# A four-layer network on one core: one-pass normalizations, biases and expert sums added by GpSimd, and a product of two weight matrices

## The chip, the cores and the metric

One core of one Trainium2 chip runs the whole network as one program. The metric is the device time in microseconds. The engines are named as the profile names them: PE (matrix products; PEld loads their weights), DVE (VectorE), ACT (ScalarE), POOL (GpSimd) and SP (which issues the transfers). PE writes its results to PSUM, in eight banks of 512 columns of float32; POOL works on SBUF only.

## What is computed

x has 4 sequences of 1024 tokens with 128 channels, in float32. Eight blocks follow one another, and each adds to x what it makes of the normalized x:

```
def _layernorm(x, axis=-1, eps=1e-05):
    m = jnp.mean(x, axis=axis, keepdims=True)
    v = jnp.var(x, axis=axis, keepdims=True)
    return (x - m) / jnp.sqrt(v + eps)
...
    x = x + _L0_attn_ref(_layernorm(x, axis=-1), ...)   # delta rule, 8 heads
    x = x + _L0_ffn_ref(_layernorm(x, axis=-1), ...)    # 128 -> 512, sines, relu, 512 -> 128, + b2
    x = x + _L1_attn_ref(_layernorm(x, axis=-1), ...)   # a small MLP trained on k, v; then applied to q
    x = x + _L1_ffn_ref(_layernorm(x, axis=-1), ...)    # 8 experts, all computed, gated
    x = x + _L2_attn_ref(_layernorm(x, axis=-1), ...)   # normalizes once more, then 8 heads
    x = x + _L2_ffn_ref(_layernorm(x, axis=-1), ...)
    x = x + _L3_attn_ref(_layernorm(x, axis=-1), ...)   # 16 heads
    x = x + _L3_ffn_ref(_layernorm(x, axis=-1), ...)    # 8 experts, the best 2
    return x
```

The parts that the change touches, besides the normalizations:

```
_L0_ffn_ref:  return jnp.einsum('bsf,fd->bsd', act, W2) + b2
_L1_attn_ref: q = x @ W_Q
              return silu(q @ W1 + b1) @ W2 + b2        # W1, b1, W2, b2 as trained
_L1_ffn_ref:  for e in range(E):
                  out = out + weights[:, e:e + 1] * (x @ expert_w[e] + expert_b[e])
_L2_attn_ref: xn = (x - mu) * jax.lax.rsqrt(var + LN_EPS) * gamma + beta
```

## The kernel before

x stays in SBUF for the whole program as `self.x`, 128 tokens on the partitions, 32 such tiles of 128 channels. `self.xnT` holds the normalized x with the channels on the partitions; `tok(t, n)` names n of its columns from tile t on.

A normalization runs over 4 batches of 8 tiles (`ln_batch`). For each tile DVE takes the statistics (`bn_stats` and `bn_aggr`, L82 and L83); ACT takes the square root for the 8 tiles (L85), DVE the reciprocal (L86) and the offset (`nm`, L106); then ACT scales the 8 tiles one by one (L109), PE transposes them four to a PSUM bank (L120), and ACT copies each bank to `xnT` (L126). In l2_attn, whose block normalizes a second time, `twice` is set: the scaled tiles go through statistics and scaling again (`xm`), and DVE writes `xnT` with the block's scale and bias (L124). `layernorm` runs the 4 batches with pools of two buffers and four PSUM banks; the two attentions, l0_ffn, l1_attn, l2_ffn and l3_ffn call it. l1_ffn calls `ln_batch` itself, one batch ahead of its tiles.

The first attention, the rounds of l1_attn and the two attentions of layers 2 and 3 have an order written out by hand; all else is put in order by a scheduler, within what the pools' buffers allow. Every engine takes its instructions in that order.

*l0_ffn* goes through 8 groups of 512 tokens. For each of 4 chunks of 128 hidden channels PE makes `hp` (L532), ACT scales it (L536), DVE takes whole turns off (L503, L504), ACT takes the sine (L539), DVE combines (L540), ACT applies relu (L541). Then for each of the 4 tiles PE sums 4 products (L545) and a product of a row of ones with the bias `b2` (L548), and DVE adds the result to x (`add_x`, L129).

*The output of l1_attn* (L601 to L618) begins when the rounds have trained W1, b1, W2 and b2. For each of 8 groups PE makes `qp` (L607), ACT copies it (L609), PE makes `hp` (L611), ACT applies silu (L613), and for each tile PE makes a product and a bias product of one row (L616, L617), and DVE adds to x.

*l1_ffn* makes the gates of 8 tiles at a time (L923 and `weights`), then goes tile by tile (`tile_of`): PE transposes the gates (L969), ACT copies them (L971), PE makes the 8 experts' outputs in two banks (L975, three `ep` banks). DVE adds the first five, each times its gate, onto x one after the other (L984); ACT scales the other three into `sc` (L982), and PE sums them together with the gated biases in `bp`, by a product with the biases (L986) and three with the identity (L988); DVE adds `bp` to x.

Elsewhere POOL adds results to x in l2_attn (L1326), l2_ffn (L1364, L1380) and l3_attn (the output bias, L1411), and clears buffers of the attentions. In the rounds of l1_attn it makes differences (L661), in the first attention products and a bias (L283, L284, L382).

Of the kernel before, what the change touches and what calls it, by code (L numbers as in the profile page):

```python
# [9 lines left out]
F32 = mybir.dt.float32  # L10
AF = mybir.ActivationFunctionType
ALU = mybir.AluOpType
# [3 lines left out]
P = 128  # L16
# [11 lines left out]
class Net:  # L28
# [71 lines left out]
    def ln_batch(self, pool, ps, b, twice=None):  # L100
        nc = self.nc

        def scaled(src, tag):
            mv, rs = self.stats(pool, src, TPB)
            nm = pool.tile([P, TPB], F32, tag="nm", name="nm")
            nc.vector.scalar_tensor_tensor(nm, mv[:, :, 0], -1.0, rs, ALU.mult, ALU.mult)  # L106
            dst = pool.tile([P, TPB, D], F32, tag=tag, name=tag)
            for i in range(TPB):
                nc.scalar.activation(  # L109
                    dst[:, i, :], src[:, i, :], AF.Identity, bias=nm[:, i : i + 1], scale=rs[:, i : i + 1]  # L110
                )
            return dst

        xn = scaled(self.x[:, b * TPB : (b + 1) * TPB, :], "xn")
        if twice is not None:
            xn = scaled(xn, "xm")
        for q in range(TPB // 4):
            tp = ps.tile([P, 4, P], F32, tag="tp", name="tp")
            for i in range(4):
                nc.tensor.transpose(tp[:, i, :], xn[:, 4 * q + i, :], self.ident)  # L120
            dst = self.tok(b * TPB + 4 * q, 512)
            src = tp.rearrange("p a b -> p (a b)")
            if twice is not None:
                nc.vector.tensor_scalar(dst, src, twice[0], twice[1], ALU.mult, ALU.add)  # L124
            else:
                nc.scalar.copy(dst, src)  # L126
# [362 lines left out]
    def l0_ffn_load(self):  # L489
# [6 lines left out]
            b2=self.row("L0_ffn_b2"),  # L496
# [9 lines left out]
    def l0_ffn(self):  # L506
# [5 lines left out]
        with tc.tile_pool(name="f0", bufs=3) as two, tc.tile_pool(name="f0c", bufs=1) as one, tc.tile_pool(  # L512
# [15 lines left out]
            for n in range(NB * SEQ // 512):  # L528
                act = two.tile([P, NF, 512], F32, tag="act", name="act")
                for c in range(NF):  # L530
# [10 lines left out]
                    nc.scalar.activation(act[:, c, :], s, AF.Relu, bias=f["b1"][:, c : c + 1])  # L541
                for i in range(4):
                    op = po.tile([P, D], F32, tag="op", name="op")
                    for c in range(NF):
                        nc.tensor.matmul(  # L545
                            op, lhsT=act[:, c, i * P : (i + 1) * P], rhs=f["W2"][:, c, :], start=c == 0, stop=False
                        )
                    nc.tensor.matmul(op, lhsT=self.ones[0:1, :], rhs=f["b2"], start=False, stop=True)  # L548
                    self.add_x(4 * n + i, op)
# [17 lines left out]
    def l1_attn(self):  # L567
# [32 lines left out]
        with tc.tile_pool(name="l1o", bufs=2) as two, tc.tile_pool(name="l1q", bufs=2, space=PSUM) as ps:  # L600
            b2p = ps.tile([1, D], F32, tag="b2p", name="b2p", bufs=1)  # L601
            nc.tensor.transpose(b2p, B2, self.ident)
            b2r = two.tile([1, D], F32, tag="b2r", name="b2r", bufs=1)
            nc.scalar.copy(b2r, b2p)
            for n in range(NB * SEQ // 512):
                qp = ps.tile([P, 512], F32, tag="qp", name="qp")
                nc.tensor.matmul(qp, lhsT=wq, rhs=self.tok(4 * n, 512), start=True, stop=True)  # L607
                q = two.tile([P, 512], F32, tag="q", name="q")
                nc.scalar.copy(q, qp)  # L609
                hp = ps.tile([P, 512], F32, tag="hp", name="hp")  # L610
                nc.tensor.matmul(hp, lhsT=W1, rhs=q, start=True, stop=True)  # L611
                a = two.tile([P, 512], F32, tag="a", name="a")
                nc.scalar.activation(a, hp, AF.Silu, bias=B1)  # L613
                for i in range(4):
                    op = ps.tile([P, D], F32, tag="op", name="op")
                    nc.tensor.matmul(op, lhsT=a[:, i * P : (i + 1) * P], rhs=W2, start=True, stop=False)  # L616
                    nc.tensor.matmul(op, lhsT=self.ones[0:1, :], rhs=b2r, start=False, stop=True)  # L617
                    self.add_x(4 * n + i, op)  # L618
# [291 lines left out]
    def l1_ffn_load(self):  # L910
# [4 lines left out]
            self.mat("L1_ffn_expert_b"),  # L915
# [23 lines left out]
    def l1_ffn(self):  # L939
# [3 lines left out]
        gw, gb, ew, eb = self.f1  # L943
# [714 lines left out]
```

## Time and profile before

| | us |
|---|---|
| three runs: median (lowest, highest) | 2828.85 (2817.63, 2829.1) |
| the profiled execution | 2815.77 |
| its span | 2814.1 |

| engine | busy us | share of the span |
|---|---|---|
| PE | 2547.2 | 91% |
| DVE | 1829.7 | 65% |
| ACT | 1538.4 | 55% |
| POOL | 179.1 | 6% |

The span holds the eight blocks one after another; stretches of it are named by their start and end in us. A row of a table of stretches gives, for each engine, its busy time and instructions, then the clock granted to PE (1.00 is full) and the transfers. A row of the groups gives the line, the engine, the operation, output and inputs, shapes and count; then busy us and mean ns of one; then the idle time before them and what ended it. A row of the timeline gives start and duration in us first. A busy engine is one with instructions under way: it may be slow at them.

### The profile page before, as it was taken

To read this page: it belongs to the slowest core of one execution; us is meant where nothing else is said; L and a number is where in the kernel's file an instruction comes from. 1 tells how busy PE (TensorE), PEld (TensorE's weight loads), DVE (VectorE), ACT (ScalarE), POOL (GpSimd) and SP (SyncE) were. 2 spreads that over 40 slices of the span, in tenths; PEclk is the share of its full clock that TensorE was granted. 3 is DMA by queue.
4 is the path that set the end of the run, shared out by engine and by line. 5 is a ranking of instruction groups with operands and counts; after the bars stand their busy time and mean duration, and the time that the engine had idled before them with its cause. 6 is when DMAs were issued, how large, how long until landed. Compare 5 with 4: busy or idle time off the path is not lost.

```text
span 2814.1 us, 51848 instructions
## 1 busy us (share of the span) xinstructions
PE 2547.2 (91%) x20320; PEld 1278.6 (45%) x20320; DVE 1829.7 (65%) x3857; ACT 1538.4 (55%) x3486; POOL 179.1 (6%) x301
## 2 busy tenths in 40 slices
PE   5687868999989959999999769999999999999967
PEld 4455536699985523333333343333333333333356
DVE  5999657567663666667676146777776776777134
ACT  4465466655554450656566650666666666666642
POOL 6111000000000000000000050000000000000001
PEclk8698878899998965999999865999999999999968
DMA  2233220000000000000100000000000000000000
GB/s 52 63 87 76 56 59 1 1 1 2 1 2 1 1 1 15 14 13 14 21 13 10 5 0 8 8 8 11 9 9 9 8 12 8 10 8 8 4 9 24
DMA packets 116468, 46.62 MB, mean 17 GB/s; under 512 B 88402, under 2 KB 110843, under 8 KB 116220
## 3 DMA queue, kind: packets, MB, share of 16 engines
q1 hardware_dynamic: 116220, 43.25, 7.8%
q8 instruction: 163, 2.67, 0.4%
q14 instruction: 85, 0.70, 0.1%
HBM read 16.95 MB, written 12.98 MB: 11 GB/s over the span
## 4 chain that ended last, share of the span: by engine, by line
PE 63%; DVE 3%; ACT 2%; POOL 1%; issue 1%; DMA 0%; SPq 0%; POOLq 0%; DVEq 0%; ACTq 0%
PE pb L1183 30%; PE po L1205 15%; PE pa L1158 6%; PE ep L975 2%; PE tp L120 2%; PE pp L1098 1%; PE gp L923 1%; PE bp L988 1%; DVE st L82 1%; ACT xn L109 1%; PE pv L1079 1%; PE op L617 1%; PE rp L1576 0%; PE bp L986 0%; PE op L616 0%
## 5 line engine op out<-in xcount | busy, mean ns | idle before, releaser
L1187 ACT ACTIVATE es<-pb 128x512 f32<-128x512 f32 x1536 | 836.2, 594 | 558.8 <-PE pb L1183 404.2
L1183 PE MATMUL pb<-q,k 32*128 32x512 f32 x3072 | 957.6, 642 | 0.7 <-ACT es L1187 0.7
L1158 PE MATMUL pa<-k,q 32*128 32x512 f32 x3072 | 909.8, 677 | 17.5 <-DMA q<-q 15.7
L1170 DVE TENSOR_REDUCE bm<-pa 128x2 f32<-128x1024 f32 x512 | 625.6, 1225 | 274.3 <-PE pb L1183 169.5
L1205 PE MATMUL po<-es,v 128*32 128x256 f32 (+1 forms) x5760 | 480.0, 405 | 0.0
L1183 PEld LDWEIGHTS pb<-q,k 32*128 32x128 f32 x3072 | 314.7, 184 | 348.2 <-ACT es L1187 190.0
L1166 DVE TENSOR_REDUCE bm<-pa 128x16 f32<-128x1024 f32 x256 | 312.5, 1221 | 107.4 <-PE pb L1183 60.7
L1205 PEld LDWEIGHTS po<-es,v 128*32 128x32 f32 x5760 | 114.2, 108 | 543.1 <-issue 510.5
L1158 PEld LDWEIGHTS pa<-k,q 32*128 32x128 f32 x3072 | 252.3, 193 | 92.8 <-DVE bm L1170 49.5
L120 PE MATMUL tp<-ident,xn 128*128 128x128 f32 x192 | 65.8, 442 | 56.0 <-ACT xn L109 50.1
L319 DVE TENSOR_TENSOR pr<-T,L 128x31 f32<-128x31 f32 (+15 forms) x248 | 90.0, 363 | 27.5 <-DMA L<-ld 20.5
L1212 DVE COPY oT<-po 128x512 f32<-128x512 f32 x48 | 32.7, 682 | 109.1 <-PE po L1205 109.1
L322 DVE TENSOR_TENSOR T<-T,pr 128x31 f32<-128x31 f32 (+15 forms) x248 | 92.3, 372 | 8.5
L109 ACT ACTIVATE xn<-x,nm,rs 128x128 f32<-128x128 f32 x224 | 89.2, 481 | 7.6 <-DVE nm L106 7.6
L984 DVE SCALAR_TENSOR_TENSOR x<-ep,g,x 128x128 f32<-128x128 f32 x160 | 55.1, 348 | 31.3 <-ACT sc L982 21.3
L277 PE MATMUL wide<-bt,kt 32*128 32x128 f32 x512 | 31.4, 375 | 48.0 <-DVE mt L366 34.3
L120 PEld LDWEIGHTS tp<-ident,xn 128*128 128x128 f32 x192 | 34.7, 187 | 88.1 <-ACT xn L109 60.1
L729 ACT ACTIVATE w<-tr,half 128x128 f32<-128x128 f32 x128 | 47.1, 368 | 47.7 <-PE tr L727 44.9
L82 DVE BATCH_NORM_STATS2 st<-x 128x6 f32<-128x128 f32 x256 | 65.2, 265 | 11.5 <-DMA x<-in_L_attn_x_dram 4.0
L704 ACT ACTIVATE a<-hp,wb 128x128 f32<-128x128 f32 x128 | 47.1, 368 | 40.7 <-PE hp L700 39.7
L975 PE MATMUL ep<-L_ffn_expert_w,xnT 128*128 128x512 f32 x128 | 69.1, 629 | 0.0
L1457 POOL MEMSET c<- 128x512 f32 (+1 forms) x2 | 2.3, 1172 | 1021.8 <-PE tp L120 1021.8
(442 smaller groups left out, 3566.5 us busy)
## 6 DMA issues: line engine op xcount, KB each, us to landing
ld<-kk SPq DMA_DIRECT2D x128, 32.0 KB
L<-ld SPq DMA_DIRECT2D x8, 512.0 KB
td<-T SPq DMA_DIRECT2D x8, 512.0 KB
tb<-td SPq DMA_DIRECT2D x128, 32.0 KB
md<-nt SPq DMA_DIRECT2D x192, 2.0 KB
q<-md SPq DMA_DIRECT2D x192, 2.0 KB
x<-in_L_attn_x_dram SPq DMA_DIRECT2D x4, 512.0 KB
od<-o SPq DMA_DIRECT2D x32, 64.0 KB
```

Of the source, the lines that this page charges most:

```text
L82: nc.vector.bn_stats(st, src[:, i, :])
L109: nc.scalar.activation(dst[:, i, :], src[:, i, :], AF.Identity, bias=nm[:, i : i + 1], scale=rs[:, i : i + 1])
L120: nc.tensor.transpose(tp[:, i, :], xn[:, 4 * q + i, :], self.ident)
L319: nc.vector.tensor_mul(pv, T[:, 0 : j + 1, j : j + 1].to_broadcast(sh), L[:, j : j + 1, j + 1 :].to_broadcast(sh))
L322: nc.vector.tensor_sub(T[:, 0 : j + 1, j + 1 :], T[:, 0 : j + 1, j + 1 :], pv)
L975: nc.tensor.matmul(ep.rearrange("p a b -> p (a b)"), lhsT=self.tok(t), rhs=ew[:, 4 * h : 4 * h + 4, :].rearrange("p a b -> p (a b)"), star ...
L1158: nc.tensor.matmul(pa[:, j % 2, :], lhsT=st["q"][r, i * P : (i + 1) * P], rhs=st["k"][r, n * 512 : (n + 1) * 512], start=True, stop=True,)
L1166: nc.vector.tensor_reduce(out[:, :, 1:9], pa.rearrange("p j (c s) -> p j c s", c=8), axis=AX.X, op=ALU.max)
L1170: nc.vector.tensor_reduce(out[:, :, n : n + 1], pa, axis=AX.X, op=ALU.max)
L1183: nc.tensor.matmul(pb, lhsT=st["k"][r, kc * P : (kc + 1) * P], rhs=st["q"][r, n * 512 : (n + 1) * 512], start=True, stop=True,)
L1187: nc.scalar.activation(es[turn][:, j, :], pb, AF.Exp, scale=scale)
L1205: nc.tensor.matmul(po[r, cols], lhsT=vring[b % 2][:, kc, 4 * g + j, :], rhs=es[:, j, cols], start=kc == 0, stop=True, skip_group_check=True,)
```

## The change

`ln_batch` takes the statistics of a tile without `bn_aggr`; the sums and squares of 8 tiles are combined in five operations of 8 columns. Four of the 8 tiles are scaled by POOL and four by ACT. With `twice` there is one pass: the second normalization's factor is worked out from the first one's variance (six more operations of 8 columns), and ACT in place of DVE writes `xnT`.

In l0_ffn and in l1's output POOL adds the bias to four tiles of x at a time (`add_bias`), PE has no bias product, and DVE adds four tiles at once from one PSUM bank (`add_four`). In l1's output W_Q and the trained W1 are multiplied once, and a group has one product where it had two. In l1_ffn the gates of 8 tiles are transposed at once and multiplied with a block-diagonal tile of the expert biases (`biases`, two products and two `add_four` a batch), and POOL adds the three experts that ACT scaled.

```diff
@@ -98,32 +98,59 @@
                 self.ln_batch(pool, ps, b, twice)
 
     def ln_batch(self, pool, ps, b, twice=None):
+
+
         nc = self.nc
-
-        def scaled(src, tag):
-            mv, rs = self.stats(pool, src, TPB)
-            nm = pool.tile([P, TPB], F32, tag="nm", name="nm")
-            nc.vector.scalar_tensor_tensor(nm, mv[:, :, 0], -1.0, rs, ALU.mult, ALU.mult)
-            dst = pool.tile([P, TPB, D], F32, tag=tag, name=tag)
-            for i in range(TPB):
-                nc.scalar.activation(
-                    dst[:, i, :], src[:, i, :], AF.Identity, bias=nm[:, i : i + 1], scale=rs[:, i : i + 1]
-                )
-            return dst
-
-        xn = scaled(self.x[:, b * TPB : (b + 1) * TPB, :], "xn")
-        if twice is not None:
-            xn = scaled(xn, "xm")
-        for q in range(TPB // 4):
+        src = self.x[:, b * TPB : (b + 1) * TPB, :]
+
+        st = pool.tile([P, TPB, 6], F32, tag="st", name="st")
+        for i in range(TPB):
+            nc.vector.bn_stats(st[:, i, :], src[:, i, :])
+        s, d, q, rs = (pool.tile([P, TPB], F32, tag=t, name=t) for t in ("s", "d", "q", "rs"))
+        nc.vector.tensor_sub(d, st[:, :, 1], st[:, :, 4])
+        nc.vector.tensor_add(q, st[:, :, 2], st[:, :, 5])
+        nc.vector.scalar_tensor_tensor(d, d, D / 4.0, d, ALU.mult, ALU.mult)
+        nc.vector.tensor_add(q, q, d)
+        nc.vector.tensor_add(s, st[:, :, 1], st[:, :, 4])
+        if twice is None:
+            nc.scalar.activation(rs, q, AF.Sqrt, bias=self.eps, scale=1.0 / D)
+            nc.vector.reciprocal(rs, rs)
+        else:
+            nc.vector.tensor_scalar(rs, q, 1.0 / D, EPS, ALU.mult, ALU.add)
+            nc.vector.reciprocal(rs, rs)
+            nc.vector.tensor_mul(q, q, rs)
+            nc.vector.tensor_scalar(q, q, 1.0 / D, EPS, ALU.mult, ALU.add)
+            nc.vector.reciprocal(q, q)
+            nc.vector.tensor_mul(rs, rs, q)
+            nc.scalar.activation(rs, rs, AF.Sqrt)
+        nm = pool.tile([P, TPB], F32, tag="nm", name="nm")
+        nc.vector.scalar_tensor_tensor(nm, s, -0.5, rs, ALU.mult, ALU.mult)
+        xn = pool.tile([P, TPB, D], F32, tag="xn", name="xn")
+        for i in range(TPB):
+            sl, bl = rs[:, i : i + 1], nm[:, i : i + 1]
+            if i % 2:
+                nc.gpsimd.tensor_scalar(xn[:, i, :], src[:, i, :], sl, bl, ALU.mult, ALU.add)
+            else:
+                nc.scalar.activation(xn[:, i, :], src[:, i, :], AF.Identity, bias=bl, scale=sl)
+        for n in range(TPB // 4):
             tp = ps.tile([P, 4, P], F32, tag="tp", name="tp")
             for i in range(4):
-                nc.tensor.transpose(tp[:, i, :], xn[:, 4 * q + i, :], self.ident)
-            dst = self.tok(b * TPB + 4 * q, 512)
-            src = tp.rearrange("p a b -> p (a b)")
+                nc.tensor.transpose(tp[:, i, :], xn[:, 4 * n + i, :], self.ident)
+            dst = self.tok(b * TPB + 4 * n, 512)
+            src_ = tp.rearrange("p a b -> p (a b)")
             if twice is not None:
-                nc.vector.tensor_scalar(dst, src, twice[0], twice[1], ALU.mult, ALU.add)
+                nc.scalar.activation(dst, src_, AF.Identity, bias=twice[1], scale=twice[0])
             else:
-                nc.scalar.copy(dst, src)
+                nc.scalar.copy(dst, src_)
+
+    def add_bias(self, t, bias):
+
+        xs = self.x[:, t : t + 4, :]
+        self.nc.gpsimd.tensor_add(xs, xs, bias.unsqueeze(1).to_broadcast([P, 4, D]))
+
+    def add_four(self, t, ps):
+        xs = self.x[:, t : t + 4, :]
+        self.nc.vector.tensor_add(xs, ps, xs)
 
     def add_x(self, t, ps):
         self.nc.vector.tensor_add(self.x[:, t, :], ps, self.x[:, t, :])
@@ -493,7 +520,7 @@
             W2=self.load("L0_ffn_W2", W2.rearrange("(c p) d -> p c d", p=P), [P, 4, D]),
             b1=self.mat("L0_ffn_b1"), th=self.mat("L0_ffn_quantum_phases"),
             wr=self.mat("L0_ffn_quantum_weights_real"), wi=self.mat("L0_ffn_quantum_weights_imag"),
-            b2=self.row("L0_ffn_b2"),
+            b2=self.spread("L0_ffn_b2"),
         )
 
     def turns(self, pool, r, shape):
@@ -539,14 +566,15 @@
                     nc.scalar.activation(s, r, AF.Sin, scale=TWO_PI)
                     nc.vector.scalar_tensor_tensor(s, s, co[:, c : c + 1], hp, ALU.mult, ALU.add)
                     nc.scalar.activation(act[:, c, :], s, AF.Relu, bias=f["b1"][:, c : c + 1])
+                self.add_bias(4 * n, f["b2"])
+                op = po.tile([P, 4, D], F32, tag="op", name="op")
                 for i in range(4):
-                    op = po.tile([P, D], F32, tag="op", name="op")
                     for c in range(NF):
                         nc.tensor.matmul(
-                            op, lhsT=act[:, c, i * P : (i + 1) * P], rhs=f["W2"][:, c, :], start=c == 0, stop=False
+                            op[:, i, :], lhsT=act[:, c, i * P : (i + 1) * P], rhs=f["W2"][:, c, :],
+                            start=c == 0, stop=c == NF - 1,
                         )
-                    nc.tensor.matmul(op, lhsT=self.ones[0:1, :], rhs=f["b2"], start=False, stop=True)
-                    self.add_x(4 * n + i, op)
+                self.add_four(4 * n, op)
 
 
 
@@ -598,24 +626,33 @@
             with tc.If(many > 0):
                 self.l1_steps(kT, vT)
         with tc.tile_pool(name="l1o", bufs=2) as two, tc.tile_pool(name="l1q", bufs=2, space=PSUM) as ps:
-            b2p = ps.tile([1, D], F32, tag="b2p", name="b2p", bufs=1)
+
+            tp = ps.tile([P, D], F32, tag="one", name="tp", bufs=1)
+            nc.tensor.transpose(tp, wq, self.ident)
+            wqT = two.tile([P, D], F32, tag="wqT", name="wqT", bufs=1)
+            nc.scalar.copy(wqT, tp)
+            wp = ps.tile([P, D], F32, tag="one", name="wp", bufs=1)
+            nc.tensor.matmul(wp, lhsT=wqT, rhs=W1, start=True, stop=True)
+            qw = two.tile([P, D], F32, tag="qw", name="qw", bufs=1)
+            nc.scalar.copy(qw, wp)
+            b2p = ps.tile([1, D], F32, tag="two", name="b2p", bufs=1)
             nc.tensor.transpose(b2p, B2, self.ident)
             b2r = two.tile([1, D], F32, tag="b2r", name="b2r", bufs=1)
-            nc.scalar.copy(b2r, b2p)
+            nc.vector.tensor_copy(b2r, b2p)
+            bp = ps.tile([P, D], F32, tag="two", name="bp", bufs=1)
+            nc.tensor.matmul(bp, lhsT=self.ones[0:1, :], rhs=b2r, start=True, stop=True)
+            b2 = two.tile([P, D], F32, tag="b2", name="b2", bufs=1)
+            nc.vector.tensor_copy(b2, bp)
             for n in range(NB * SEQ // 512):
-                qp = ps.tile([P, 512], F32, tag="qp", name="qp")
-                nc.tensor.matmul(qp, lhsT=wq, rhs=self.tok(4 * n, 512), start=True, stop=True)
-                q = two.tile([P, 512], F32, tag="q", name="q")
-                nc.scalar.copy(q, qp)
                 hp = ps.tile([P, 512], F32, tag="hp", name="hp")
-                nc.tensor.matmul(hp, lhsT=W1, rhs=q, start=True, stop=True)
+                nc.tensor.matmul(hp, lhsT=qw, rhs=self.tok(4 * n, 512), start=True, stop=True)
                 a = two.tile([P, 512], F32, tag="a", name="a")
                 nc.scalar.activation(a, hp, AF.Silu, bias=B1)
+                self.add_bias(4 * n, b2)
+                op = ps.tile([P, 4, D], F32, tag="op", name="op")
                 for i in range(4):
-                    op = ps.tile([P, D], F32, tag="op", name="op")
-                    nc.tensor.matmul(op, lhsT=a[:, i * P : (i + 1) * P], rhs=W2, start=True, stop=False)
-                    nc.tensor.matmul(op, lhsT=self.ones[0:1, :], rhs=b2r, start=False, stop=True)
-                    self.add_x(4 * n + i, op)
+                    nc.tensor.matmul(op[:, i, :], lhsT=a[:, i * P : (i + 1) * P], rhs=W2, start=True, stop=True)
+                self.add_four(4 * n, op)
 
     def l1_rounds(self, keep, kT, vT):
 
...
@@ -940,13 +976,18 @@
 
 
         nc, tc = self.nc, self.tc
-        gw, gb, ew, eb = self.f1
+        gw, gb, ew = self.f1
         E, OWN = 8, 5
         with ExitStack() as c:
             ln = c.enter_context(tc.tile_pool(name="f1l", bufs=2))
             lps = c.enter_context(tc.tile_pool(name="f1q", bufs=2, space=PSUM))
             one = c.enter_context(tc.tile_pool(name="f1c", bufs=2))
             two = c.enter_context(tc.tile_pool(name="f1", bufs=3))
+
+            eb = one.tile([TPB * E, TPB, D], F32, tag="eb", name="eb", bufs=1)
+            nc.gpsimd.memset(eb, 0.0)
+            for i in range(TPB):
+                nc.sync.dma_start(eb[E * i : E * i + E, i, :], self.w["L1_ffn_expert_b"])
             ps = c.enter_context(tc.tile_pool(name="f1p", bufs=2, space=PSUM))
 
             def weights(b):
@@ -963,12 +1004,22 @@
                 nc.vector.tensor_mul(g, g, sm.unsqueeze(2).to_broadcast([P, TPB, E]))
                 return g
 
+            def biases(b, g):
+
+                ap = ps.tile([TPB * E, P], F32, tag="ap", name="ap", bufs=1)
+                nc.tensor.transpose(ap, g.rearrange("p t e -> p (t e)"), self.ident)
+                gT = one.tile([TPB * E, P], F32, tag="gT", name="gT")
+                nc.scalar.copy(gT, ap)
+                for n in range(TPB // 4):
+                    bp = ps.tile([P, 4, D], F32, tag="bp", name="bp", bufs=1)
+                    nc.tensor.matmul(
+                        bp.rearrange("p a b -> p (a b)"), lhsT=gT,
+                        rhs=eb[:, 4 * n : 4 * n + 4, :].rearrange("p a b -> p (a b)"), start=True, stop=True,
+                    )
+                    self.add_four(b * TPB + 4 * n, bp)
+
             def tile_of(t, g):
                 xs = self.x[:, t, :]
-                ap = ps.tile([P, P], F32, tag="ap", name="ap", bufs=1)
-                nc.tensor.transpose(ap[0:E, :], g, self.ident)
-                gT = two.tile([E, P], F32, tag="gT", name="gT")
-                nc.scalar.copy(gT, ap[0:E, :])
                 eps = []
                 for h in range(2):
                     ep = ps.tile([P, 4, D], F32, tag="ep", name="ep", bufs=3)
@@ -982,17 +1033,15 @@
                     nc.scalar.mul(sc[:, e - OWN, :], eps[e // 4][:, e % 4, :], g[:, e : e + 1])
                 for e in range(OWN):
                     nc.vector.scalar_tensor_tensor(xs, eps[e // 4][:, e % 4, :], g[:, e : e + 1], xs, ALU.mult, ALU.add)
-                bp = ps.tile([P, D], F32, tag="bp", name="bp", bufs=1)
-                nc.tensor.matmul(bp, lhsT=gT, rhs=eb, start=True, stop=False)
                 for e in range(OWN, E):
-                    nc.tensor.matmul(bp, lhsT=self.ident, rhs=sc[:, e - OWN, :], start=False, stop=e == E - 1)
-                self.add_x(t, bp)
+                    nc.gpsimd.tensor_add(xs, xs, sc[:, e - OWN, :])
 
             self.ln_batch(ln, lps, 0)
             g = weights(0)
             for b in range(NB):
                 if b + 1 < NB:
                     self.ln_batch(ln, lps, b + 1)
+                biases(b, g)
                 for i in range(TPB):
                     tile_of(b * TPB + i, g[:, i, :])
                     if i == TPB // 2 and b + 1 < NB:
```

More of the change, by code (lines that the diff above doesn't have):

```diff
@@ L914, in l1_ffn_load @@
             self.load("L1_ffn_expert_w", ew.rearrange("e d f -> d e f"), [D, 8, D]),
-            self.mat("L1_ffn_expert_b"),
         )
```

## The prediction

> **What bounds the kernel now.** I began with the table of stretches, cut at the stages.
>
> ```profile
> core 0: us, PE busy (x) PEld busy (x) DVE busy (x) ACT busy (x) POOL busy (x), PEclk, DMA share, GB/s
> 403.00:465.00 62.00, 60.60 (x302) 40.92 (x303) 51.12 (x104) 48.18 (x80) 0.00 (x0) 1.00 0.00 1
> 837.00:893.00 56.00, 44.23 (x163) 26.67 (x163) 14.91 (x77) 15.14 (x24) 0.00 (x0) 0.85 0.00 1
> 893.00:1005.00 112.00, 111.87 (x491) 65.47 (x491) 69.50 (x268) 52.37 (x170) 0.00 (x0) 0.92 0.00 1
> 1005.00:1052.00 47.00, 17.36 (x54) 8.56 (x53) 31.86 (x162) 30.73 (x80) 0.69 (x2) 0.58 0.00 1
> 1052.00:1590.00 538.00, 531.22 (x4116) 182.59 (x4116) 339.37 (x321) 287.98 (x521) 13.37 (x14) 0.94 0.08 13
> 1690.00:2676.00 986.00, 980.61 (x8144) 336.21 (x8144) 673.85 (x684) 576.43 (x1070) 0.00 (x0) 0.97 0.06 8
> ```
>
> The two attentions (538 and 986 us), the rounds (337) and the first attention (363) make 2,224 of 2,814 us; the diff leaves their instructions alone. What can move is some 400 us: l0_ffn (403:465), l1's output (837:893) and l1_ffn (893:1005), where PE is full and POOL idle, and the normalizations (as 1005:1052), where no engine is full and one waits for another.
>
> Then the groups of l1's output and of l1_ffn, for who holds PE:
>
> ```profile
> L617 PE MATMUL op<-b2r,ones 1*128 1x128 f32 x64 | 16.4, 338 | 0.0
> L616 PE MATMUL op<-wb,a 128*128 128x128 f32 x64 | 15.3, 323 | 0.9 <-ACT a L613 0.9
> ```
> ```profile
> L975 PE MATMUL ep<-L_ffn_expert_w,xnT 128*128 128x512 f32 x118 | 61.1, 608 | 0.0
> L984 DVE SCALAR_TENSOR_TENSOR x<-ep,g,x 128x128 f32<-128x128 f32 x145 | 50.4, 349 | 28.6 <-ACT sc L982 20.4 <-PE ep L975 4.1
> L988 PE MATMUL bp<-sc,ident 128*128 128x128 f32 x180 | 25.3, 275 | 0.0
> L986 PE MATMUL bp<-L_ffn_expert_b,gT 8*128 8x128 f32 x60 | 14.6, 323 | 0.0
> ```
>
> One-row bias products (L617) cost PE as much as the full ones beside them, and L986 and L988 take 40 us of PE in l1_ffn for sums that another engine could make.
>
> Last, POOL's own rows and what happens when DVE runs beside it (timeline of l2_ffn):
>
> ```profile
> L661 POOL TENSOR_TENSOR df<-dh 128x128 f32<-128x128 f32 x32 | 14.6, 457 | 324.4 <-DVE dh L754 324.4
> L382 POOL TENSOR_TENSOR x<-x,L_attn_ln_b 128x512 f32<-128x512 f32 x8 | 11.2, 1407 | 0.0
> ```
> ```profile
> 1627.68 1.42 DVE L1355 SCALAR_TENSOR_TENSOR m<-xnT,L_ffn_mu_r,m 128x1024 f32<-128x1024 f32 x1 [3.72 <-ACT m L1354]
> ...
> 1630.22 2.32 DVE L1355 SCALAR_TENSOR_TENSOR m<-xnT,L_ffn_mu_k,m 128x1024 f32<-128x1024 f32 x1
> ...
> 1631.44 2.22 POOL L1380 TENSOR_TENSOR x<-x,r 128x512 f32<-128x512 f32 x1
> ...
> 1632.46 0.68 DVE L1378 TENSOR_TENSOR r<-vp,r 128x512 f32<-128x512 f32 x1
> ```
>
> With two SBUF inputs on both engines each slows (1.42 to 2.32, 1.28 to 2.22 us). L1378, which takes one input from PSUM, ran in 0.68 beside that same POOL add. The DVE work that will run beside POOL is mostly of the second kind (add_four, L540, L984); in l0_ffn L504 is of the first.
>
> **The change part by part.** Times are against the profiled execution, 2815.8 us (span 2814.1 and 1.7 around it), 13 us under the median of the runs, 2828.85. Under 0.5% (14 us) a measurement of this kernel can't tell from no change.
>
> *l0_ffn body.* A group of 512 tokens takes 10.3 us now (396.2 to 482.6 for eight, PE full). The 4 bias products L548 go, at 0.42 us each and with them the broken rhythm of the 16 products L545, which by themselves pace at 0.22: PE falls to 4 x 0.86 + 16 x 0.22 = 7.0. ACT has 4 x (0.59 + 0.52 + 0.61) = 6.9 (quiet durations), DVE 4 x 1.6 (starts of L503, L504 and L540 at 0.34, 0.61 and 0.65 behind one another) and one add_four of 0.69 = 7.1, POOL 1.41, which can cost DVE as much again where it meets L504. Three engines at 7 that feed one another don't reach 7: I take 8.5, so 8 x 1.8 = 14 (5 to 20).
>
> *l1's output.* Now 5.04 us a group: 2 x 0.86 for qp and hp and 8 products at 0.415. After: 0.86 + 4 x 0.22 = 1.74, eight times 14 us; POOL's adds (8 x 1.39 = 11) and DVE's (8 x 0.69) fit beside it. Ahead stands the new chain transpose, copy, product, copy, some 2 us, and the Silu table load (1.28) that is there now. The stage starts at half clock, as now. 843 to 888 becomes 843 to 866: 22 (12 if PE stays at half clock, 25).
>
> *l1_ffn.* Now 3.01 us a tile, all PE: L975 1.72, L986 0.42, L988 0.67, the gates' transpose 0.11 and the rest. After, PE has 1.72 and its share of transposes, gates and biases, 2.1. DVE has 160 L984 at a pace of 0.38 = 61 us and some 10 of normalization, gates and biases: 2.2 a tile. POOL has 3 adds, which pace at 0.48 where one follows the other (L283 to L284), and half an xn: 1.64. DVE binds: 32 x 2.2 = 71 where 909 to 1009.8 is 101, a gain of 30. But l2_attn's statistics now run in this stream as x gets ready, 24 bn_stats of 0.2 and three sets of eleven small operations of 0.2, 11 us in all, and they wait for POOL's last add of their tile. I take 22 (0 to 30).
>
> *l2_attn's normalization.* Now 42 us after the last tile (1009.8 to 1052.1): four times statistics, xn, statistics, xm, transposes, L124, each waiting for the one before. The second pass goes (32 L109 of 0.48, 32 statistics and moments at 0.26 a tile, one table wait), the first stats lie in l1_ffn. What is left is 32 transposes at half clock, 12.7 us, the last batch's chain of about 6, and table loads: 20 to 22. Gain 20 (10 to 28).
>
> *The other normalizations.* A batch is now held by ACT: 8 xn at 0.40 and two copies at 0.58 = 4.3 us. POOL takes four xn. A one-input 128x128 on POOL isn't in the trace; the nearest rows are a copy at 0.29 and the two-input add at 0.46; I take 0.4, and 0.8 if DVE disturbs it, where POOL's four end with ACT's eight today. ACT falls to 2.8 us a batch, but transposes at half clock take 3.2. l1 gains 5 (2 to 7). In l0_ffn the last batch's xn stand on POOL behind six bias adds of 1.4, so 2 of 5 remain. In l2_ffn xn stands behind L1326 (2.36), in l3_attn between the adds L1411 (2.34 each): 5 and 4; l3_ffn 4 (together 13, from 5 to 20). The moments swap eight bn_aggr of 0.17 for five operations of 0.16 to 0.25: no gain and no loss.
>
> The broadcast of b2 and the eight loads of the expert biases on SP come long before their use; GpSimd's memset of that tile has 16 us before biases. Cost nothing, 2 us at most.
>
> Sum: 2 + 14 + 5 + 22 + 22 + 20 + 13 = 98 us. The profiled execution would be 2718, on the median's footing 2731; I say 2725.
>
> The Trainium skill ("GPSIMD Engine Reference", introduction and section 1) speaks against the change: it calls GpSimd the wrong choice for elementwise arithmetic, where VectorE is about twice as fast, and says that its SBUF interfaces are shared with VectorE's instructions of two SBUF inputs. The trace agrees on both (457 ns against the 292 of the 128x128 add L129 on DVE, and the 2.32 above).
>
> **The rivals.**
>
> *POOL becomes the bound.* If its adds stretch by the 1.73 of L1380, from 0.48 to 0.83 us, and xn to 0.8, a tile of l1_ffn takes 3 x 0.83 + 0.4 = 2.9 and l1_ffn gains (101 - 93) 8. The backlog delays l2_attn's statistics (gain 10 for 20), and xn at 0.8 takes the other normalizations' 20. l0_ffn and l1 keep 36: 54 in all, 2768 (midway between the two footings, as all that follow). It decides from 0.6 us an add. For: x[t] is shared with add_four and with small two-input operations. Against: L1378's 0.68, and the 457 of L661 in a busy stage.
>
> *Waits in place of PE.* The stages become chains over four engines: l0_ffn's group 9.5 for 8.5 (6 kept), l1_ffn's tile 2.6 (10 kept), l1 15, l2 15, the rest 10: 56, 2766. For: DVE, ACT and PE within 0.2 us of each other in l0_ffn. Against: three ep banks and eight PSUM banks let PE run ahead.
>
> *The clock.* A PE no longer full may lose its grant.
>
> ```profile
> 897.00:907.00 10.00, 10.00 (x31) 6.69 (x31) 4.09 (x18) 5.30 (x12) 0.00 (x0) 0.50 0.01 2
> ```
> ```profile
> 2802.00:2808.00 6.00, 3.28 (x33) 2.54 (x31) 1.12 (x3) 0.44 (x2) 1.45 (x2) 1.00 0.00 0
> ```
>
> The first row is busy at half clock, the second half idle at full, so busy time alone doesn't decide. Four 512-column products took 3.1 us at half clock, 1.8 times the 1.72. All of l0_ffn and l1_ffn at that rate: 12.6 a group (18 lost), 3.8 a tile (25 lost); l1 still gains 12, the normalizations 40: 9 us faster, 2813, no change.
>
> The Trainium skill ("TensorE: Matmul & The Clock Gate", part 1) grants full clock after one busy window of about 3.4 us and takes it after an idle one; by that rule l1_ffn keeps it and the sum stands. The first row differs: ten busy microseconds didn't bring it.
>
> *Slower: one POOL add costs 2 us in l1_ffn*, for its waits on ACT and DVE and the shared port. 32 x (3 x 2.1 + 0.2) = 208 us for 101 loses 107 against the 76 gained elsewhere: 31 slower, 2853. It decides from 1.8 us an add. Only the 128x1024 add (2.34) is so long; 457 speaks against.
>
> **How the numbers follow.** Forecast 0.55, POOL bound 0.17, waits 0.18, clock 0.05, slower 0.05. Faster by over 0.5%: 0.90, same 0.05, slower 0.05. The range takes in the first three with the spread of their terms, 2690 to 2785.
>
> **What would show it.** In the profile after: l1's output some 23 us long with L617 gone; l1_ffn with DVE at 90% or more and PE at 1.00 clock; POOL's 128x128 add near 0.46; 20 us from l1_ffn's last add to the first product of the attention. An add at 0.8, or DVE below 80% in l1_ffn, makes a rival right; a change in the attentions' 1,524 us by over 10 makes the frame wrong.

## The result and the profile after

The changed kernel took 2721.49 us (median of four runs, 2719.78 to 2725.73) against 2827.24 us before, a ratio of 0.964 with an interval of 0.9614 to 0.9665. By the ratio that is 102 us faster (95 to 109); the two medians are 106 apart. The forecast was 2725. Its profiled execution spans 2721.3 us, 92.8 less than the one before.

The table cuts both profiles at the same instructions: the first xn, the first hp (L532, now L559), the last full product of the groups (L545; the bias product behind it counts to the next stretch), the first projection of layer 1, the transpose of b2 behind the rounds, the last full product of l1's output (L616), the first and last sum of an expert (L984, now L1035), the first product of l2_attn, and so on. A stretch is the difference of two start times. The column "alone" is from four kernels below.

| stretch, us | before | after | difference | forecast | alone |
|---|---|---|---|---|---|
| l0_ffn, normalization | 19.6 | 16.3 | -3.3 | -2 | 14.1 |
| l0_ffn, groups | 85.2 | 75.5 | -9.7 | -14 | 71.0 |
| l1, normalization | 23.5 | 17.9 | -5.6 | -5 | 17.8 |
| l1, output | 43.8 | 18.7 | -25.1 | -22 | 19.3 |
| l1_ffn up to the first expert sum | 18.5 | 24.9 | +6.4 | | 23.2 |
| l1_ffn, first to last expert sum | 104.2 | 79.6 | -24.6 | -22 for both | 77.2 |
| l2_attn, normalization | 42.8 | 10.9 | -31.9 | -20 | 11.0 |
| the attentions and l2_ffn, with the last three normalizations | 1659.9 | 1650.5 | -9.4 | -13 | |
| what the diff leaves alone | 816.6 | 827.0 | +10.4 | 0 | |

The last row is the time up to the first xn (376.6, 381.2), the projections and rounds of layer 1 (337.9, 341.6) and the end from l3_ffn's first gates on (102.1, 104.2). Those moved by as much between kernels that don't touch them: the first xn came between 376.2 and 382.5 in all the profiles of this study. The gain by the ratio, 102, is nearer to the sum of the stretches that changed, 103, than to the difference of the two spans.

The table of stretches of the changed kernel, l0_ffn's groups without their ends, l1's output, l1_ffn and l2_attn's normalization:

```profile
core 0: us, PE busy (x) PEld busy (x) DVE busy (x) ACT busy (x) POOL busy (x), PEclk, DMA share, GB/s
406.00:476.00 70.00, 59.41 (x312) 42.39 (x310) 57.17 (x110) 54.05 (x90) 1.27 (x6) 0.93 0.00 1
831.00:853.00 22.00, 19.03 (x86) 11.89 (x86) 6.87 (x15) 7.31 (x11) 9.85 (x8) 0.84 0.01 3
876.10:955.70 79.60, 74.59 (x185) 30.28 (x183) 64.14 (x256) 39.46 (x120) 46.86 (x105) 0.94 0.00 1
955.70:966.60 10.90, 5.86 (x32) 4.32 (x32) 4.55 (x25) 9.28 (x18) 5.91 (x14) 0.74 0.01 3
```

PE is still the fullest engine of l1_ffn, 74.6 of 79.6 us; DVE is at 81%, not at 90. In the last row the clock is not at half throughout: its mean is 0.74.

The groups of l1's output (64 entries for 32 products, most of them 0.11 us from one to the next, and no L617), and of l1_ffn's tiles, then POOL's three new rows in the whole program:

```profile
L654 PE MATMUL op<-wb,a 128*128 128x128 f32 x64 | 8.3, 281 | 0.0
```
```profile
L1026 PE MATMUL ep<-L_ffn_expert_w,xnT 128*128 128x512 f32 x122 | 60.9, 632 | 3.3 <-DVE x L1035 3.0
L1035 DVE SCALAR_TENSOR_TENSOR x<-ep,g,x 128x128 f32<-128x128 f32 x160 | 49.5, 342 | 13.1 <-ACT sc L1033 8.1 <-PE ep L1026 4.2
```
```profile
L132 POOL TENSOR_SCALAR xn<-x,rs,nm 128x128 f32<-128x128 f32 x112 | 48.8, 449 | 1259.1 <-DMA oc<-oT 992.5 <-DVE q L113 116.8 <-DMA sc<-oT 88.7
L1037 POOL TENSOR_TENSOR x<-x,sc 128x128 f32<-128x128 f32 x96 | 43.6, 454 | 34.3 <-DVE x L1035 23.6 <-DVE sm L1002 5.8
L149 POOL TENSOR_TENSOR x<-x,L_ffn_b 128x512 f32<-128x512 f32 x8 | 9.9, 1259 | 0.0
```

POOL's adds did not stretch: 454 ns where the rounds' adds took 457. Nor did L1035, 342 ns for 348 before.

### The profile page after: what moved, and what is told of

Read it like the earlier page. It is cut to its first block, busy times and chain, and to the rows that moved or that the text cites. A ratio compares the mean times of both kernels' runs of the same rounds, so it can differ in the third digit from the quotient of the medians.

```text
span 2721.3 us, 50960 instructions
## 1 busy us (share of the span) xinstructions
PE 2465.4 (91%) x19913; PEld 1232.3 (45%) x19913; DVE 1809.7 (67%) x3643; ACT 1484.3 (55%) x3315; POOL 292.8 (11%) x526
## 4 chain that ended last, share of the span: by engine, by line
PE 62%; DVE 4%; ACT 1%; POOL 1%; issue 1%; DMA 0%; SPq 0%; POOLq 0%; DVEq 0%; ACTq 0%
PE pb L1232 31%; PE po L1254 16%; PE pa L1207 5%; PE ep L1026 2%; PE pp L1147 1%; PE tp L138 1%; PE gp L959 1%; PE pv L1128 1%; DVE st L108 1%; PE rp L1625 1%; DVE bm L1219 0%; DVE x L1035 0%; PE bp L1015 0%; PE pr L1480 0%; PE hp L648 0%
## 5 line engine op out<-in xcount | busy, mean ns | idle before, releaser
L132 POOL TENSOR_SCALAR xn<-x,rs,nm 128x128 f32<-128x128 f32 x112 | 48.8, 449 | 1259.1 <-DMA oc<-oT 992.5
L138 PE MATMUL tp<-ident,xn 128*128 128x128 f32 x224 | 52.6, 401 | 63.0 <-ACT xn L134 50.3
L349 DVE TENSOR_TENSOR T<-T,pr 128x31 f32<-128x31 f32 (+15 forms) x248 | 92.8, 374 | 8.5
L464 PE MATMUL sp<-ux,kn 128*128 128x256 f32 x128 | 50.5, 532 | 17.8 <-ACT ux L453 17.7
L749 DVE TENSOR_TENSOR dlt<-gr,mask 128x128 f32<-128x128 f32 x96 | 28.0, 292 | 48.6 <-PE gr L747 48.3
L1035 DVE SCALAR_TENSOR_TENSOR x<-ep,g,x 128x128 f32<-128x128 f32 x160 | 49.5, 342 | 13.1 <-ACT sc L1033 8.1
```

What stands on the lines that cost most here:

```text
L138: nc.tensor.transpose(tp[:, i, :], xn[:, 4 * n + i, :], self.ident)
L349: nc.vector.tensor_sub(T[:, 0 : j + 1, j + 1 :], T[:, 0 : j + 1, j + 1 :], pv)
L464: mm(sp[:, g].rearrange("p a b -> p (a b)"), lhsT=kns[c % len(kns)][:, 4 * g : 4 * g + 4, :].rearrange("p a b -> p (a b)"), rhs=ux[:, g].r ...
L1035: nc.vector.scalar_tensor_tensor(xs, eps[e // 4][:, e % 4, :], g[:, e : e + 1], xs, ALU.mult, ALU.add)
```

## The experiments

Twelve kernels ran. The theory to be tested was that the gain is the sum of parts that stand by themselves, with the two large misses of the forecast (l2_attn's normalization, l0_ffn's groups) due to the PE clock and to ACT's table loads. The main rival was that the parts make one another's gain.

**One part alone.** Four kernels, each the one before with one part of the diff: `ln_batch` only; `l0_ffn` (with `spread` for b2) only; the output part of `l1_attn` only; `l1_ffn` and its load only.

> The kernel before with the new normalization alone. Theory 'parts stand by themselves': the stretches between the same instructions of the two profiles give the normalizations 3.3 (l0_ffn) + 5.6 (l1) + 31.9 (l2_attn) + 2.7 + 2.4 + 4.3 = 50 us, so about 2777 against 2827 before, with some 11 us from l1_ffn's last sum to the first product of l2_attn. Rival 'the l2 gain is made by the lighter l1_ffn': while PE is full in l1_ffn the early statistics only lengthen it or come late; l2_attn's normalization gains half, and the time is about 2793.

> The kernel before with l0_ffn's bias on GpSimd and add_four alone. Parts by themselves: 9.7 us off the eight groups, 2817. Rival: the forecast's 14 us (2813), if the new normalization ahead of it cost it something, for instance the bias adds that stood among POOL's xn.

> The kernel before with the output of l1_attn alone: W_Q times W1 once, the bias on GpSimd, add_four. Parts by themselves: 24.8 us, 2802. Rival: part of it is only moved, since the next normalization starts with the PE clock down either way: 15 us, 2812.

> The kernel before with l1_ffn's biases and three expert sums on GpSimd alone. Parts by themselves: 18.2 us, 2809. Rival 'the slow start is the normalization's': from the last add of l1_attn to the first expert sum the changed kernel took 24.9 us for 18.5; if that comes from the new normalization's order, this kernel has the gain of the tiles alone, 104.2 - 79.6 = 24.6 us, 2802.

Beside the same runs of before (median 2818.72), the ratios were 0.9828 (0.9802 to 0.9854), 0.9961 (0.9948 to 0.9973), 0.9908 (0.9885 to 0.9931) and 0.9949 (0.9932 to 0.9967): 48.5, 11.0, 25.9 and 14.4 us. Together 99.8, against 102 for all of them. In sum the parts stand by themselves, as far as the intervals go: they leave some 10 us open. Within l0_ffn they do not, as the second point shows. Three things follow from the stretches:

- l2_attn's normalization takes 11.0 us with the new `ln_batch` alone, where l1_ffn is as full as before (first to last expert sum 105.0 us). The rival, that the lighter l1_ffn makes that gain, falls.
- l0_ffn's groups take 71.0 us alone, the 14 of the forecast, so here the rival of that run holds. All parts together lose 4.5 of them, and 2.2 of the normalization ahead (14.1 alone, 16.3 together). Of such differences not all are effects: in the kernel with l1_ffn alone the groups, which that part doesn't touch, took 88.6 us for 85.2.
- The slow start of l1_ffn is mostly its own: 23.2 us with the old normalization, 20.9 with the new normalization alone, 18.5 before. The tiles alone took 77.2 us.

**Late statistics.** What l2_attn's early statistics are worth:

```diff
+        if twice is not None:
+            for i in range(TPB):
+                nc.vector.tensor_copy(st[:, i, :], self.x[:, NT - 1, 0:6])
         for i in range(TPB):
             nc.vector.bn_stats(st[:, i, :], src[:, i, :])
```

> The changed kernel, with l2_attn's statistics kept out of l1_ffn: DVE fills each column of st with six values of the last tile of x before bn_stats overwrites it (32 copies of about 0.1 us each), so none can start before that tile is done. Theory 'early statistics keep PE at full clock': the stretch from the last expert sum to l2_attn's first product was 10.9 us with the 32 transposes at full clock (16 in 1.97 us); now PE idles over 3 us, its clock is halved, and the stretch is 20 to 24 us, while l1_ffn gets 2 us shorter: 8 to 11 us slower than the changed kernel's 2721, 2731. Rival 'one pass is all of it': 11 to 14 us for the stretch, 2722.

Ratio 0.9663 (0.964 to 0.9686), median 2727.06; the interval overlaps that of the changed kernel, so the reading rests on the stretches. The stretch to the first product went from 10.9 to 22.4 us, the tiles from 79.6 to 77.1. Its rows, the stretch and PE's timeline in it:

```profile
953.00:975.40 22.40, 8.14 (x32) 5.43 (x32) 14.62 (x114) 14.34 (x30) 9.13 (x21) 0.52 0.01 1
```
```profile
951.44 0.59 PE L1029 MATMUL ep<-L_ffn_expert_w,xnT 128*128 128x512 f32 x1
961.90 1.97 PE L141 MATMUL tp<-ident,xn 128*128 128x128 f32 x8 [9.87 <-ACT xn L137]
```

PE idles for 9.87 us, the clock is at half (0.52) and eight transposes take 1.97 us. In the changed kernel PE had transposes to do at once, at full clock, sixteen in the same time; the other sixteen came at half clock:

```profile
956.09 1.97 PE L138 MATMUL tp<-ident,xn 128*128 128x128 f32 x16 [1.76 <-DVE x L1035]
960.62 1.93 PE L138 MATMUL tp<-ident,xn 128*128 128x128 f32 x8 [2.57 <-ACT xn L134]
963.80 1.97 PE L138 MATMUL tp<-ident,xn 128*128 128x128 f32 x8 [1.25 <-ACT xn L134]
```

The forecast's 20 to 22 us come close to this kernel's 22.4, though not by their terms: 32 transposes at half clock took 8.1 us, not 12.7. In the kernel before, eight took 3.16, because ACT, which made their input alone, needs 3.18 for eight:

```profile
1047.49 3.18 ACT L109 ACTIVATE xm<-xn,nm,rs 128x128 f32<-128x128 f32 x8 [0.56 <-DVE nm L106]
1048.03 3.16 PE L120 MATMUL tp<-ident,xm 128*128 128x128 f32 x8 [6.25 <-ACT xm L109]
```

That PE loses its full clock after a pause is what the Trainium skill ("TensorE: Matmul & The Clock Gate", part 1) says of an idle window of some 3.4 us. Here less was enough: the clock was kept over a pause of 1.76 us, and from 961 on, behind one of 2.57 us, it was at half (0.50). Of the 31.9 us, at most 11.5 belong to the early start, since the 32 copies, 3.7 us of DVE, lie in this stretch too. PE's transposes took 8.1 us for 5.9, so most of the 11.5 is the chain of statistics behind the last tile and not the clock. The other 20 us belong to the single pass and what goes with it.

**The three adds on VectorE.**

```diff
-                    nc.gpsimd.tensor_add(xs, xs, sc[:, e - OWN, :])
+                    nc.vector.tensor_add(xs, xs, sc[:, e - OWN, :])
```

> The changed kernel, with the three adds of an expert tile moved from GpSimd to VectorE. Theory 'DVE sets the tile and POOL relieves it almost for nothing': three adds of 0.25 to 0.29 us lengthen the tile from 2.49 to about 3.3 us; l1_ffn takes 24 us more, 2745. Rival 'POOL's adds disturb DVE by about what they take off it': L1035 gets faster without them, and it is under 8 us.

Ratio 0.9696 (0.9674 to 0.9718), 2734.37. Slower than the changed kernel by some 16 us, between the two theories, and neither held. The tiles took 83.0 us, 3.4 more; the stretch to l2_attn's first product 19.7, 8.7 more, since l2_attn's statistics no longer found room among the tiles (2 bn_stats in 78 us of tiles, where the changed kernel had 24). L1035 took 345 ns without POOL beside it, 342 with. So POOL's adds did not slow L1035. DVE got 26.2 us of adds in the tiles, which grew by 3.4: it had room in them, though part of that room is what the statistics left.

**Four experts to GpSimd.**

```diff
-        E, OWN = 8, 5
+        E, OWN = 8, 4
```

> The changed kernel, with four experts on VectorE and four scaled by ACT and added by GpSimd. Theory 'DVE sets the tile': DVE loses 32 instructions at 0.38, 12 us of its stream, POOL gets 32 adds of 0.47, 2.1 us a tile and still under DVE: tiles 70 to 72 us for 79.6, 2713. Rival 'PE with its three ep banks sets it, POOL's last add comes later': under 2 us either way, and the stretch to l2_attn's first product, 10.9 us, gets longer.

Ratio 0.9642 (0.9619 to 0.9666), 2718.08: no change. The tiles took 80.7 us for 79.6. DVE has less to do and waits, for PE and for POOL:

```profile
876.00:956.70 80.70, 75.67 (x188) 30.77 (x188) 57.87 (x229) 47.37 (x153) 61.51 (x138) 0.91 0.00 1
```
```profile
L1035 DVE SCALAR_TENSOR_TENSOR x<-ep,g,x 128x128 f32<-128x128 f32 x124 | 41.7, 344 | 13.6 <-PE ep L1026 12.3
L108 DVE BATCH_NORM_STATS2 st<-x 128x6 f32<-128x128 f32 x32 | 8.5, 283 | 7.3 <-POOL x L1037 7.3
```

Of the 7.3 us for POOL, 5.0 lie within the tiles. In the changed kernel the statistics there (L108) waited for nothing:

```profile
L108 DVE BATCH_NORM_STATS2 st<-x 128x6 f32<-128x128 f32 x24 | 6.7, 281 | 0.0
```

DVE went from 64.1 to 57.9 us of work, PE stayed at 75.7 of 80.7; with the three adds on DVE, PE was at 74.4 too. So DVE alone does not set the tile. That PE alone does is not shown either, for the total is a sum of gains and losses. By batches of eight tiles this kernel took 21.4, 18.6, 19.5 and 21.2 us, the changed kernel 23.5, 20.4, 18.3 and 17.4. It won 3.9 us in the first two, some 2 of them by a clock that was full 5 us sooner (estimate: half of what it ran less at half clock). It lost 5.0 in the last two, where DVE's statistics wait for POOL's last add and the clock dips again (0.57 from 950.0 to 956.7). That is the rival's second half: POOL's last add comes later. In the changed kernel, and with the adds on DVE, the clock is 0.94 over the tiles since the first 10 us or so run at half; here it is 0.91.

**All xn on ACT.** The branch for odd tiles taken out of `ln_batch`.

> The changed kernel, with all eight xn of a batch on ACT. Theory 'POOL's share makes the gain of the single normalizations': ACT again holds a batch at 8 x 0.40 + 2 x 0.58 = 4.3 us, l1's normalization goes from 17.9 back to some 22 us, and five others lose 2 to 4: 12 to 16 us slower, 2735. Rival 'the order of waits made it, not POOL': within 4 us of 2721.

Ratio 0.9714 (0.969 to 0.9739), 2739.83. l1's normalization took 23.6 us (17.9), l0's 18.9 (16.3), l2_attn's 13.5 (10.9), the stretches with l2_ffn's, l3_attn's and l3_ffn's 0.3, 2.8 and 2.8 more. POOL's share is the gain of most plain normalizations: without it, nothing is left of l1's 5.6 and 0.7 of l0's 3.3. For l2_ffn's it is not shown: its stretch holds over 500 us of attention, which moved by up to 6 us between kernels that share it.

**The biases behind the tiles.** `biases(b, g)` moved behind the loop over the batch's tiles.

> The changed kernel, with the expert biases of a batch added to x behind its tiles, not ahead of them. From l1's last product to the first expert sum the changed kernel takes 24.9 us, 18.5 before. Theory 'the sum of biases is the new first link': transposed gates, copy, two products and the add stand ahead of the first L1035; behind the tiles they cost nothing, 19 to 21 us and a time 4 us under 2721. Rival 'table loads and the half clock make the start': no change beyond 1 us.

Ratio 0.9661 (0.9644 to 0.9678), 2726.46: not faster; that it is slower rests on the stretches, for the intervals overlap. The start did shrink, from 24.9 to 21.2 us, and more came back: tiles 86.6 for 79.6, the stretch behind them 14.2 for 10.9. DVE's add now waits for POOL's sums of its four tiles, and the one `bp` bank keeps PE waiting for DVE:

```profile
885.78 0.69 DVE L153 TENSOR_TENSOR x<-bp,x 128x512 f32<-128x512 f32 x1 [0.99 <-POOL x L1037]
```
```profile
L1015 PE MATMUL bp<-eb,gT 64*128 64x512 f32 x15 | 8.9, 669 | 6.7 <-DVE x L153 6.7
```

**l0_ffn's missing 4.5 us.** Before, ACT's sine table was loaded inside the normalization, behind its last square root, for the sine of l0_ffn's coefficients (L522). In the changed kernel the scheduler put that sine (now L549) ahead of the square roots, so that the table has to be loaded a second time, behind the scalings of three chunks and ahead of the first chunk's sine (L566). The load of the kernel before, then the first of the changed kernel:

```profile
390.44 1.28 ACT L522 ACT_TABLE_LOAD   x1
```
```profile
374.20 1.28 ACT L549 ACT_TABLE_LOAD   x1 [5.28 <-DMA on<-od]
```

Three kernels. The first delays the bias adds and loads the table early:

```diff
+            sin = one.tile([P, 4], F32, tag="sin", name="sin")
+            nc.scalar.activation(sin, self.tok(NT - 1, 4), AF.Sin, scale=0.0)
+            b2 = one.tile([P, D], F32, tag="b2", name="b2")
+            nc.vector.scalar_tensor_tensor(b2, self.tok(NT - 1), 0.0, f["b2"], ALU.mult, ALU.add)
...
-                self.add_bias(4 * n, f["b2"])
+                self.add_bias(4 * n, b2)
```

The second has only the two lines of `sin`. The third has these two, and the bias as one-row products on PE again, with no add on POOL.

> The changed kernel, with l0_ffn's order mended by two data dependencies: the bias tile is made by DVE from the last normalized tile (times 0, plus b2), so that POOL's eight adds stand behind all of its xn; and a sine of 4 columns of that tile times 0 loads ACT's sine table in the gap before the first chunk. Theory 'l0_ffn's missing 4.5 us and the normalization's 2.2 are the late table load with the clock dip behind it and the bias adds ahead of xn': normalization 14.1 for 16.3, groups 71 for 75.5, 6.7 us off, 2715. Rival 'the groups are longer because POOL's adds and the new order hold DVE': the adds now lie beside the groups, which stay at 75 or more; 2 us or less.

> The changed kernel, with only the sine of 4 columns of the last normalized tile (times 0) added, so that ACT loads its sine table in the gap before the first chunk; POOL's bias adds stay among its xn. Theory 'the late table load and the clock dip behind it cost the groups 4.5 us': normalization 16.3 as in the changed kernel, groups 71, 4.5 us under it, 2717 where it has 2721. Rival 'it is POOL's adds beside the first chunks, or the new order': groups 75 again, no change.

> The changed kernel, with l0_ffn's bias back on PE (a product of one row for each tile, add_four kept), no POOL add there, and the early sine table. If POOL's adds cost in whichever place they stand (2.2 us ahead of xn; L531 at 1.64 for 0.69 beside the groups), the normalization takes 14.1 and the groups are set by PE at 4 x 0.86 + 16 x 0.22 + 4 x 0.42 = 8.6 us, 71 to 73 in all: 5 to 6 us under the changed kernel, 2715, the best of the orders tried. Rival 'the bias products break PE's rhythm': the groups go back to 80 and more, 2725 or above.

| | normalization | groups | ratio to before (interval) |
|---|---|---|---|
| changed kernel | 16.3 | 75.5 | 0.964 (0.9614 to 0.9665) |
| late adds, early sine | 14.2 | 74.7 | 0.9628 (0.9601 to 0.9654) |
| early sine alone | 16.3 | 70.3 | 0.9614 (0.9601 to 0.9627) |
| bias on PE, early sine | 13.1 | 87.5 | 0.9658 (0.9638 to 0.9677) |

The early sine alone gives 5.2 us: the late load was on the path. The second load in the changed kernel, and ACT's timeline in the kernel with the early sine alone, where the load ends before the first chunk:

```profile
402.90 1.28 ACT L566 ACT_TABLE_LOAD   x1
```
```profile
396.78 1.28 ACT L556 ACT_TABLE_LOAD   x1
398.08 0.20 ACT L556 ACTIVATE sin<-xnT 128x4 f32<-128x4 f32 x1
398.99 0.69 ACT L565 ACTIVATE r<-hp,ang 128x512 f32<-128x512 f32 x1 [0.70 <-PE hp L561]
```

The load itself is 1.28 us. Behind it the clock of the changed kernel dipped again (0.74 from 409.5 to 413.5, where the other kernels stood at 1.00); that this makes the rest of the 5.2 was not tried by itself.

In the late-add kernel the normalization is rid of its 2.2 us, as expected, and the groups gain nothing, since DVE now meets POOL's adds. Seven of POOL's adds, 1.44 us each on average, and DVE's first instructions:

```profile
391.95 10.05 POOL L149 TENSOR_TENSOR x<-x,b 128x512 f32<-128x512 f32 x7
393.26 1.45 DVE L530 TENSOR_SCALAR rnd<-r 128x512 f32<-128x512 f32 x1 [2.62 <-ACT r L567]
394.75 1.64 DVE L531 TENSOR_TENSOR r<-r,rnd 128x512 f32<-128x512 f32 x1
...
400.79 1.39 DVE L571 SCALAR_TENSOR_TENSOR s<-s,co,hp 128x512 f32<-128x512 f32 x2
```

L530 takes 0.42 and L531 0.69 when POOL is quiet. Each now lasts about as long as one of POOL's adds, and these stretch too, from 1.26 us to 1.44 and up to 1.71. L571, which reads PSUM, keeps its pace. The Trainium skill ("GPSIMD Engine Reference", section 1) names just these two kinds as the ones that contend, DVE instructions of two SBUF inputs or in a two-port mode; L530 has one input, so its 1.45 would be the second.

With the bias on PE the groups go back to 87.5 us, longer than before: the rival of that run. The 32 one-row products, 17 us more than in the second kernel, are what l0_ffn's gain comes from.

The kernel with the early sine alone has the lowest ratio of those tried. Its interval overlaps that of the changed kernel, so what the two lines bring rests on the 5.2 us of the profile more than on the times. Its profile is also 7.5 us shorter from l2_attn's first product to l3_ffn's gates (1643.0 for 1650.5), where the two lines change nothing.

## Why the prediction was right

Its total was right, and part of that is luck. l2_attn's normalization gave 12 us more than forecast; l1_ffn, l0_ffn's groups and the last three normalizations gave 12 less.

- *l1's output* (22): 25.1. The two groups of a pair take 3.75 us, 1.87 each where 1.74 was forecast. The terms written out, 14 + 2 + 1.3 us, come near the 18.7 that the stage took; the 23 that were forecast hold some 6 more for a start at half clock, of which the first four `hp` showed 1.9 (3.74 us for 1.88).
- *l1_ffn* (22): 18.2. The tiles gave 24.6, more than the 22 forecast, and the start took 6.4 back. The step that failed in the tiles is "DVE binds". Its 160 sums were priced at a pace of 0.38 us, 61 in all; in the changed kernel they mostly come 0.26 us apart (the row below) and hold DVE for 49.5, so that with the statistics it was busy for 64.1, 2.0 a tile. What makes the two paces was not tried. PE was busy for 74.6, 2.3 a tile for the 2.1 forecast; the first 9.8 us, up to 886, ran at half clock, and without that it would be 2.2 (estimate: half of the 9.8 taken off). The longer start was not in the sum: gates, transpose, copy, product and add now stand ahead of the first L1035, where the bias used to come last. Moving the biases behind the tiles takes 3.7 us off the start, and the new normalization alone makes it 2.4 longer.

```profile
932.47 1.10 DVE L1035 SCALAR_TENSOR_TENSOR x<-ep,g,x 128x128 f32<-128x128 f32 x4
```

- *l2_attn's normalization* (20, range 10 to 28): 31.9, outside its range. The mis-sized term is "32 transposes at half clock, 12.7 us" behind the last tile: they took 5.9. The 12.7 were the pace at which ACT alone had made their input; with POOL's help eight take 1.97 us at half clock. And half of them ran at full clock, as early statistics had made their input ready.
- *l0_ffn's groups* (14): 9.7, and 14.2 by itself. The forecast read the work of the groups and not the table load, which the old order hid and the new one puts ahead of the first sine. (Its 10.3 us a group is not the eighth of the 86.4 that stand beside it, which is 10.8.)
- *l0_ffn's normalization* (2 of 5): 3.3 of 5.5. That POOL's bias adds would stand ahead of xn was right, and costs 2.2 us (16.3 against 14.1).
- *The other plain normalizations* (5 and 13): 5.6 and 9.4. xn on POOL took 449 ns, 0.43 us apart (eight in 3.45), for the 0.4 that was taken.
- *The rivals.* "POOL becomes the bound" asked for adds of 0.6 us and more in l1_ffn: they took 454 ns. Its mechanism is real, and shows at L530 and L531 above, which work from SBUF alone, not where DVE reads PSUM. The pair that the prediction read for it, L1380 at 1.28 and 2.22 us, is no clean one: the add of 1.28 (1630.17) lay beside the same L1355 of 2.32. "The clock" did not take the tiles: 0.94 over all of them, after a start at half, which cost PE some 5 us (the estimate above). "Waits in place of PE" gave 9.5 us for a group of l0_ffn, and 75.5 / 8 is 9.4, in part for the table load; it gave 2.6 for a tile of l1_ffn, and 79.6 / 32 is 2.5, with PE busy for 94% of it. Both are nearer than the forecast's 8.5 and 2.2: what it had wrong is l1's output, at 15 us, and the normalizations.

## What to carry to other kernels

A sum on PE that only adds a bias, or adds tiles with an identity, is worth moving to an idle engine where PE is full, but look at what DVE does beside it: here an add on POOL cost nothing next to DVE work that reads PSUM (L1035, L571), and about 1 us of its 1.4 next to L530 and L531, from SBUF to SBUF. Not all work from SBUF suffers: `bn_stats`, with one input, took 281 ns among POOL's adds and 265 before. When a stage becomes shorter, look for what the old order hid: a table load, a first link of a chain, another engine that set the pace of the transposes. Statistics that can start under the stage before were worth up to 11.5 us here, where the single pass and what goes with it brought 20.

## What the runs showed of the hardware that was not expected

- A DVE operation of 8 columns with two SBUF inputs can be held until POOL's adds end: `nm` took 1.97 us, up to 394.29, in l0_ffn's last batch, where four bias adds ran from 389.35 to 394.27; its median in the program is 0.17:

```profile
392.32 1.97 DVE L127 SCALAR_TENSOR_TENSOR nm<-s,rs 128x8 f32<-128x8 f32 x1
```

- A `tensor_scalar` of 128x128 with two column operands on POOL takes 449 ns, as long as an add of two tiles (454), not nearer to a copy (291).
